# A two-layer graph attention kernel: sines in pairs later, weight matrices earlier, and the normalised rows' stores on another queue

## The chip, the cores and the metric

The kernel runs on one core of a Trainium2 chip. The metric is the time on the device in microseconds, the median of several runs. A profile is one execution of its own, recorded instruction by instruction; its durations are used for the working, and its total is not the median of the timed runs.

## The reference, cut to what matters

There are N = 6250 nodes with 128 features, and E = 106250 edges sorted by their target node (`dst`). Two transformer convolutions follow each other, with a normalisation over all nodes between them and a layer norm over the sum with x at the end.

```python
def _transformer_conv(h, edge_attr, src, dst, Wq, bq, Wk, bk, Wv, bv, We, Ws, bs):
    q, k, v = ...                      # h @ W + b, two heads of 64
    e = (edge_attr @ We).reshape(-1, H, C)
    kj = k[src] + e
    alpha = einsum('ehc,ehc->eh', q[dst], kj) / sqrt(C)
    a = softmax of alpha over the edges of each dst
    out = segment_sum((v[src] + e) * a[:, :, None], dst, num_segments=n)
    return out.reshape(n, H * C) + h @ Ws + bs

rel_t = last_update[src] - t
rel_t_enc = cos(rel_t[:, None] * time_w[None, :] + time_b)      # 32 values an edge
edge_attr = concatenate([rel_t_enc, msg], axis=-1)              # 32 + 64
h = _transformer_conv(x, edge_attr, src, dst, ...layer 1...)
h = relu((h - mean over nodes) / sqrt(var over nodes + 1e-5) * bn_g + bn_b)
h = _transformer_conv(h, edge_attr, src, dst, ...layer 2...)
x = layernorm(x + h)
```

## The kernel before, in words

**Tiling.** The edges are cut into NC = 106 chunks of CE = 1024 edges, each with the edges of at most NN = 64 nodes. A chunk lies in SBUF as eight tiles of 128 edges (`ff`, 241 columns). Instead of q, k and v of each edge, the kernel makes for each node a column per head (the "table", `ftab`), against which the raw features of the source nodes and the edge attributes are multiplied. The tables are made in 13 blocks of 512 nodes (`tables`, lines 622 to 638) as products of small matrices with the node features; `matrices` (574 to 605) makes these matrices from the weights once for each layer: three transposes (L580), then four pairs of products (L595 a matrix, L599 a column), each emptied from PSUM by ACT (L597) and DVE (L601).

**A round.** `conv(c, extra, first_blocks)` runs over both layers (c = 0 and 1) with a loop over k from -4 to NC + 2. The order of instructions on each engine is the order in which the program issues them (`manual_schedule`). Round k holds, for different chunks: `fetch(k + 4)`, which has SP read the chunk's node and edge offsets (L722, L723) and issue its loads (edge attributes L725, table L736, in layer 2 also the encodings `fz` L739, the turned attributes `fxT` L741 and the residual rows `fr` L743); `gather(k + 4)`, eight indirect loads by POOL (L748); `score(k, 0)` and `score(k, 1)` on PE (L817, L818); `turn_weights(k - 1)`, transposes and ACT copies (L840, L841); `divide(k - 2)` on DVE (L852 to L855); `finish_turn(k - 2)` (L867, L868, L870); `lowest(k)` on DVE (L823, L825); `turn_in(k + 1)` (L797 to L807); `weigh(k)`, the exponential on ACT (L830); in layer 1 the encoding of times; a pull of the generator `extra`; `finish(k - 2)`; and `gather_sums(k - 1)` on PE (L847). PE's transposes in `turn_in`, `turn_weights` and in the extra work share four PSUM banks in rotation.

**Sines.** `encode` makes the arguments of the cosine of one chunk on DVE (L765 to L773), `sine` has ACT evaluate them (L779), `place` copies them into the chunk and has SP store them for layer 2 (L784, L785). Up to round SINGLE = 16 each round encodes chunk k + 2 and takes its sine at once. In round SINGLE it encodes both k + 2 and k + 3. From then on it encodes chunk k + 3 and takes one sine for two chunks. ACT loads another function table whenever it goes from exponentials to a sine and back; a load stands in the profile at the line of the function that needs it.

**Extra work of layer 1.** `rest()` is a generator from which each round pulls one step, two steps in rounds 0 to 3 and after round 80. It makes the table blocks 1 to 12 (five steps each, then two in which weights for layer 2 are loaded by `load_others`, while it has any), then layer 2's matrices (seven steps), then for each of 13 blocks of 512 rows `pass_rows`: turn the rows of the finished layer back (L1002, L1004), take their statistics (L992) and store them in `h_d` from SP's queue (L1012, L1014). A block of rows waits for the round in which its last node is finished.

**The seam between the layers.** After layer 1, scale and shift are worked out (L1035 to L1044), and block 0 of the table of layer 2 is made. Then `conv(1, ...)` begins. At k = -4 it fetches and gathers chunk 0, and calls `first_blocks`: ACT normalises the other 12 blocks of `fhT` in place (L1074), PE turns each block of 512 nodes into rows (L1002), DVE copies them out of PSUM into one of three buffers `fhr` (L1004), and they are stored in `hn_d` (L1012, the last 106 rows by L1014), in the kernel before from ACT's queue. Chunks 0 to 2 (k < RAW = 3) gather their rows from `h_d`, not normalised, and are normalised by ACT while they are turned (L799). Chunks from 3 on gather from `hn_d`, so POOL's gather of chunk 3 needs all its stores landed.

Of the kernel before, what the change touches and what calls it, by code (L numbers as in the profile page):

```python
# [13 lines left out]
P = 128  # L14
# [646 lines left out]
def ordered(ctx: ExitStack, tc: tile.TileContext, pl, x, dst, edge_attr_64, conv2, bn_g, bn_b, out):  # L661


    nc = tc.nc
    N = x.shape[0]
# [26 lines left out]

    AHEAD = 4

    SINGLE = 16

    RAW = 3

    def conv(c, extra, first_blocks=None):
# [221 lines left out]
        def pull(gen, n):  # L921
            for _ in range(n):
                next(gen, None)

        with cs, tc.manual_schedule():
            for k in range(-AHEAD, NC + 3):
                def on(j):
                    return 0 <= j < NC

                if on(k + AHEAD):  # L930
                    fetch(k + AHEAD)
                    gather(k + AHEAD)
                if k == -AHEAD and c:
                    first_blocks()
                if on(k):
                    score(k, 0)
                if on(k - 1):
                    turn_weights(k - 1)
                place()
                if on(k - 2):  # L940
                    divide(k - 2)
                if on(k):
                    score(k, 1)
                if on(k - 2):
                    finish_turn(k - 2)
                if on(k):
                    lowest(k)
                if on(k + 1):
                    turn_in(k + 1, 0)
                if on(k):  # L950
                    weigh(k)
                if on(k + 1):
                    turn_in(k + 1, 1)
                for j in (k + 2,) if k < SINGLE else (k + 2, k + 3) if k == SINGLE else (k + 3,):
                    if c == 0 and on(j):
                        encode(j)
                        if j < SINGLE + 3:
                            sine()
                if k >= 0:
                    at_round[0] = k  # L960
                    pull(extra, 2 if k < 4 or k > 80 else 1)
                if len(args) == 3 or args and k == NC - 4:
                    sine()
                if on(k - 2):
                    finish(k - 2)
                if c and on(k):
                    if k < RAW:
                        normalise(k)
                    nc.vector.tensor_copy(ch[k].f[:, :, 1 + D:1 + D + TD], ch[k].z)
                for _ in range(min(len(done), 2 if k > NC - 12 else 1)):  # L970
                    store(*done.pop(0))
                if on(k - 1):
                    gather_sums(k - 1)
            at_round[0] = 2 * NC
            for _ in extra:
                pass
            for rows in done:
                store(*rows)
# [4 lines left out]
    with tc.tile_pool(name="fpw", bufs=2) as pw:  # L983
        with tc.tile_pool(name="ftp", bufs=3, space=bass.MemoryType.PSUM) as mp, tc.manual_schedule():
            turn_features(nc, pl, mp, N)

        def pass_rows(b0):

            r0 = b0 * GE
            n = min(GE, N - r0)  # L990
            rows = turned_rows(b0)
            nc.vector.bn_stats(stats[:, b0], hT[:, r0:r0 + n])  # L992
            yield
            put_rows(nc.sync, h_d, b0, rows)
            yield

        def turned_rows(b0):
            r0 = b0 * GE
            n = -(-min(GE, N - r0) // P)
            pt = pl.bank().rearrange("p (b d) -> p b d", d=P)  # L1000
            for i in range(n):
                nc.tensor.transpose(pt[:, i], hT[:, r0 + i * P:r0 + (i + 1) * P], ident)  # L1002
            rows = pw.tile([P, GE // P, P], F32, name="fhr", bufs=3)
            nc.vector.tensor_copy(rows[:, :n], pt[:, :n])  # L1004
            return rows

        def put_rows(eng, to, b0, rows):
            r0 = b0 * GE
            n = min(GE, N - r0)
            full = n // P  # L1010
            if full:
                eng.dma_start(to[r0:r0 + full * P, :].rearrange("(b p) d -> p b d", p=P), rows[:, :full])  # L1012
            if n > full * P:
                eng.dma_start(to[r0 + full * P:N, :], rows[:n - full * P, full])  # L1014

        def rest():
            others = load_others(nc, pl, const, conv2, bn_g, bn_b)
            for b0 in range(1, NT):
                yield from tables(nc, pl, 0, xT[:, b0 * GE:(b0 + 1) * GE], b0, pw, lambda: pl.bank())

                for _ in range(2):
                    next(others, None)
                    yield
            yield from matrices(nc, pl, 1, const, lambda: pl.bank()[:, :P])
            for b0 in range(-(-N // GE)):

                while at_round[0] < 3 + max(k for k in range(NC) if first(k)[0] < (b0 + 1) * GE):
                    yield
                yield from pass_rows(b0)

        conv(0, rest())


        moments = const.tile([P, 2], F32, name="fmom")
        nc.vector.bn_aggr(moments, stats)  # L1035
        std = const.tile([P, 1], F32, name="fstd")
        nc.vector.tensor_scalar(std, moments[:, 1:], EPS, None, op0=OP.add)
        nc.scalar.activation(std, std, AF.Sqrt)
        scale = pl.scale = const.tile([P, 1], F32, name="fscale")
        nc.vector.reciprocal(scale, std)  # L1040
        nc.vector.tensor_mul(scale, scale, pl.bng)
        shift = pl.shift = const.tile([P, 1], F32, name="fshift")
        nc.vector.tensor_mul(shift, scale, moments[:, 0:1])
        nc.vector.tensor_sub(shift, pl.bnb, shift)  # L1044

        def residual(b0):

            r0 = b0 * GE
            xr = pw.tile([P, 4, D], F32, name="fxr")
            n = min(GE, N - r0)  # L1050
            full = n // P
            if full:
                nc.scalar.dma_start(xr[:, :full], x[r0:r0 + full * P, :].rearrange("(b p) d -> p b d", p=P))
            if full < 4:
                nc.vector.memset(xr[:, full:], 0.0)
                nc.scalar.dma_start(xr[:n - full * P, full], x[r0 + full * P:N, :])
            yield
            pg = pl.bank().rearrange("p (b d) -> p b d", d=D)
            for i in range(4):
                nc.tensor.matmul(pg[:, i], hT[:, r0 + i * P:r0 + (i + 1) * P], pl.ws[1], start=True, stop=True)  # L1060
            nc.vector.tensor_add(xr, xr, pg)
            nc.vector.tensor_add(xr, xr, pl.bs2[:, None, :].to_broadcast([P, 4, D]))
            nc.scalar.dma_start(res_d[r0:r0 + GE, :].rearrange("(b p) d -> p b d", p=P), xr)

        def block(b0):
            res = residual(b0)
            next(res)
            yield from tables(nc, pl, 1, hT[:, b0 * GE:(b0 + 1) * GE], b0, pw, lambda: pl.bank())
            next(res, None)
            yield  # L1070

        def relu(b0):
            r = slice(b0 * GE, (b0 + 1) * GE)
            nc.scalar.activation(hT[:, r], hT[:, r], AF.Relu, bias=shift, scale=scale)  # L1074

        def first_blocks():

            for b0 in range(1, NT):
                relu(b0)
            for b0 in range(-(-N // GE)):  # L1080
                put_rows(nc.scalar, hn_d, b0, turned_rows(b0))

        with tc.tile_pool(name="fpp2", bufs=3, space=bass.MemoryType.PSUM) as pp, tc.manual_schedule():
            pl.bank = lambda: pp.tile([P, GE], F32, name="fpg")
            relu(0)
            for _ in block(0):
                pass

            diag = const.tile([P, 2, P], F32, name="fdiag")
            spread = pl.spread = const.tile([P, 2, P], F32, name="fspread")  # L1090
            pb = pp.tile([P, 2, P], F32, name="fpb", bufs=1)
            for i, col in enumerate((scale, shift)):
                nc.vector.tensor_scalar(diag[:, i], ident, col, None, op0=OP.mult)
                nc.tensor.matmul(pb[:, i], pl.ones, diag[:, i], start=True, stop=True)
            nc.vector.tensor_copy(spread, pb)

        def rest():
            for b0 in range(1, NT):
                yield from block(b0)
                yield  # L1100
                yield

        conv(1, rest(), first_blocks)
# [214 lines left out]
```

## Time and profile before

| | us |
|---|---|
| median of 3 runs | 2816.28 (2807.70 to 2822.51) |
| the profiled execution, its own time | 2308.59 |
| its span, first to last instruction | 2306.8 |
| mean granted TensorE clock in it | 0.980 |
| layer 1, rounds 0 to 105 (exponentials) | 67.3 to 1178.3 |
| seam, from the last exponential of layer 1 to the first of layer 2 | 1178.3 to 1241.1 |
| layer 2, first exponential to the last | 1241.1 to 2283.9 |

How to read it: PE is TensorE's matmuls and PEld its weight loads, DVE is VectorE, ACT ScalarE, POOL GpSimd, SP SyncE. `L817` is line 817 of the kernel. A row such as `fps<-fft,ftab` names the tile written and those read. "Idle before" in brackets is the time that an engine stood still ahead of an instruction, with the work that ended it. The profiled execution is shorter than the timed runs by 18%; the working below says how the two are set against each other.

### The profile page before, as it was taken

Reading aid. Unit: us, or ns where it says so; the run is one execution under the profiler, and the core shown is the slowest. Engines: PE = TensorE matmul, PEld = TensorE weight load, DVE = VectorE, ACT = ScalarE, POOL = GpSimd, SP = SyncE. Lnnn points to the kernel's source line nnn. Section 1 sums busy time; section 2 is a strip of 40 time slices with the busy share of each in tenths; the row PEclk is TensorE's granted clock in tenths of the full one; section 3 lists DMA queues with packets and bytes.
Section 4 is the critical chain, followed back from the end, with each engine's and each line's share of the span. In section 5 each row is a group of like instructions: output and inputs, shape, how many; then the busy total and the mean of one; then the engine's idle time right before and its main releaser. Section 6 shows DMA issues by size and latency. Waiting matters only on the chain. (4 is left out here: it accounts for less than half of the span.)

```text
span 2306.8 us, 39033 instructions
## 1 busy us (share of the span) xinstructions
PE 2214.9 (96%) x11586; PEld 1711.8 (74%) x11586; DVE 1240.1 (54%) x3738; ACT 1195.2 (52%) x1919; POOL 1629.7 (71%) x1717
## 2 busy tenths in 40 slices
PE   5999999999999999999977999999999999999997
PEld 3688788888887888788854777777777777776775
DVE  5676676767676767687734343434343334433333
ACT  3677565656666665555642344444444444443444
POOL 3777777777777777677616777777777777777772
PEclk7999999999999999999997999999999999999999
DMA  7666566666666566566628766677666776666561
GB/s 233 170 179 177 155 180 187 174 160 179 189 174 183 156 191 178 134 184 177 161 87 233 188 179 174 180 185 189 183 179 173 185 189 178 177 161 163 156 156 39
DMA packets 431067, 396.58 MB, mean 172 GB/s; under 512 B 279649, under 2 KB 375134, under 8 KB 427518
## 3 DMA queue, kind: packets, MB, share of 16 engines
q1 hardware_dynamic: 351188, 236.53, 37.0%
q0 software_dynamic: 54656, 113.07, 20.4%
q10 hardware_dynamic: 25002, 44.40, 5.5%
q8 instruction: 95, 1.56, 0.3%
q14 instruction: 126, 1.03, 0.1%
HBM read 277.19 MB, written 113.17 MB: 169 GB/s over the span
## 5 line engine op out<-in xcount | busy, mean ns | idle before, releaser
L748 POOL DMA_INDIRECT ff<-xv_d,fsrcs x848 | 819.3, 966 | 313.5 <-issue 220.9
L748 POOL DMA_INDIRECT ff<-hn_d,fsrcs x824 | 782.6, 950 | 261.6 <-issue 216.4
L847 PE MATMUL fpa<-ff,fpt 128*128 128x225 f32 x3392 | 694.9, 357 | 0.0
L847 PEld LDWEIGHTS fpa<-ff,fpt 128*128 128x128 f32 x3392 | 628.9, 190 | 11.8 <-issue 1.0
L841 ACT COPY fpt<-fppt 128x512 f32<-128x512 f32 x424 | 227.7, 589 | 503.8 <-PE fppt L840 492.4
L817 PE MATMUL fps<-fft,ftab 128*128 128x512 f32 x848 | 443.5, 605 | 3.7 <-ACT fft L799 2.1
L801 ACT COPY fft<-fpx 128x512 f32<-128x512 f32 x418 | 243.3, 582 | 365.7 <-PE fpx L797 365.7
L870 DVE COPY fat<-fpo 128x256 f32<-128x256 f32 x212 | 90.1, 425 | 590.1 <-PE fpo L868 584.3
L830 ACT ACTIVATE fs<-fps,fm 128x1024 f32<-128x1024 f32 x212 | 236.3, 1115 | 84.3 <-DVE fm L825 81.8
L840 PEld LDWEIGHTS fppt<-fident,fs 128*128 128x128 f32 x1696 | 198.5, 140 | 104.8 <-issue 104.3
L797 PE MATMUL fpx<-fident,ff 128*128 128x128 f32 x1696 | 248.2, 276 | 20.1 <-DMA ff<-hn_d,fsrcs 11.2
L823 DVE TENSOR_REDUCE flow<-fps 128x1 f32<-128x1024 f32 x212 | 257.5, 1215 | 11.4 <-PE fps L818 11.4
L797 PEld LDWEIGHTS fpx<-fident,ff 128*128 128x128 f32 x1696 | 198.6, 142 | 31.8 <-DMA ff<-hn_d,fsrcs 19.1
L840 PE MATMUL fppt<-fident,fs 128*128 128x128 f32 x1696 | 220.1, 272 | 0.0
L818 PE MATMUL fps<-fxT,ftab 112*128 112x512 f32 x424 | 218.4, 596 | 0.0
L818 PE MATMUL fps<-fet,ftab 112*128 112x512 f32 x424 | 217.1, 593 | 0.0
L817 PEld LDWEIGHTS fps<-fft,ftab 128*128 128x128 f32 x848 | 166.6, 226 | 7.4 <-ACT fs L830 3.3
L818 PEld LDWEIGHTS fps<-fet,ftab 112*128 112x128 f32 x424 | 106.3, 251 | 75.8 <-issue 58.2
L818 PEld LDWEIGHTS fps<-fxT,ftab 112*128 112x128 f32 x424 | 84.1, 198 | 99.9 <-issue 99.2
L772 DVE SCALAR_TENSOR_TENSOR farg<-fturns,farg 128x256 f32<-128x256 f32 x318 | 135.4, 426 | 10.9
L852 DVE TENSOR_SCALAR finv<-fpa 128x1 f32<-128x1 f32 x212 | 32.5, 153 | 196.1 <-DMA ff<-hn_d,fsrcs 88.7
L806 PE MATMUL fpe<-fident,ff 128*112 128x128 f32 x848 | 130.1, 277 | 2.8 <-DVE ff L784 1.5
(202 smaller groups left out, 2309.0 us busy)
## 6 DMA issues: line engine op xcount, KB each, us to landing
ff<-in_edge_attr SPq DMA_DIRECT2D x212, 256.0 KB
et_d<-fet SPq DMA_DIRECT2D x106, 448.0 KB
fxT<-et_d SPq DMA_DIRECT2D x106, 448.0 KB
ftab<-tab_d SPq DMA_DIRECT2D x106, 192.0 KB
tab_d<-fo ACTq DMA_DIRECT2D x13, 1536.0 KB
ff<-xv_d,fsrcs POOLq DMA_INDIRECT x848
enc_d<-fzs SPq DMA_DIRECT2D x106, 128.0 KB
ftab<-tab_d SPq DMA_DIRECT2D x106, 128.0 KB
```

The lines of the kernel that those rows point to most:

```text
L748: nc.gpsimd.indirect_dma_start(out=f[:, t, (1 if c else 0):1 + D], out_offset=None, in_=(h_d if k < RAW else hn_d) if c else pl.xv_d, in_o ...
L772: nc.vector.scalar_tensor_tensor(arg, turn, -part, arg, op0=OP.mult, op1=OP.add)
L797: nc.tensor.transpose(px[:, t * P:(t + 1) * P], s.f[:, u * 4 + t, 1:1 + D], ident)
L801: nc.scalar.copy(s.ft[:, u * GE:(u + 1) * GE], px)
L806: nc.tensor.transpose(pe[:EC, t * P:(t + 1) * P], s.f[:, u * 4 + t, 1 + D:], ident)
L817: nc.tensor.matmul(s.ps[:, w], s.tab[:, :, 0], s.ft[:, w], start=True, stop=False)
L818: nc.tensor.matmul(s.ps[:, w], s.tab[:EC, :, 1], s.et[:, w], start=False, stop=True)
L823: nc.vector.tensor_reduce(low, s.ps, AX.X, OP.min)
L830: nc.scalar.activation(s.s, s.ps, AF.Exp, bias=s.bias, scale=-1.0)
L840: nc.tensor.transpose(pp[:, t * P:(t + 1) * P], s.s[:, at:at + P], ident)
L841: nc.scalar.copy(s.pt[:, u * GE:(u + 1) * GE], pp)
L847: nc.tensor.matmul(s.pa, s.pt[:, t * P:(t + 1) * P], s.f[:, t, 1:1 + D + EW], start=t == 0, stop=t == T - 1)
```

## The change

SINGLE goes from 16 to 40. The matrices of layer 2 are made in the steps that `load_others` leaves empty between the table blocks, not after them; and rounds pull two steps after round 96 only, not after round 80. `put_rows` issues all its stores from SP's queue, those of `hn_d` too, which come in the program after the loads of chunk 0 and ahead of those of chunk 1; and it cuts the last 106 rows into two stores of 96 and 10.

```diff
-    SINGLE = 16
+    SINGLE = 40
...
-                    pull(extra, 2 if k < 4 or k > 80 else 1)
+                    pull(extra, 2 if k < 4 or k > 96 else 1)
...
-            put_rows(nc.sync, h_d, b0, rows)
+            put_rows(h_d, b0, rows)
...
-        def put_rows(eng, to, b0, rows):
+        def put_rows(to, b0, rows):
             r0 = b0 * GE
             n = min(GE, N - r0)
             full = n // P
             if full:
-                eng.dma_start(to[r0:r0 + full * P, :].rearrange("(b p) d -> p b d", p=P), rows[:, :full])
-            if n > full * P:
-                eng.dma_start(to[r0 + full * P:N, :], rows[:n - full * P, full])
+                nc.sync.dma_start(to[r0:r0 + full * P, :].rearrange("(b p) d -> p b d", p=P), rows[:, :full])
+
+            left = n - full * P
+            for a, b in ((0, left // 16 * 16), (left // 16 * 16, left)):
+                if a < b:
+                    nc.sync.dma_start(to[r0 + full * P + a:r0 + full * P + b, :], rows[a:b, full])
 
         def rest():
-            others = load_others(nc, pl, const, conv2, bn_g, bn_b)
+            def second():
+                yield from load_others(nc, pl, const, conv2, bn_g, bn_b)
+                yield from matrices(nc, pl, 1, const, lambda: pl.bank()[:, :P])
+
+            others = second()
             for b0 in range(1, NT):
                 yield from tables(nc, pl, 0, xT[:, b0 * GE:(b0 + 1) * GE], b0, pw, lambda: pl.bank())
 
                 for _ in range(2):
                     next(others, None)
                     yield
-            yield from matrices(nc, pl, 1, const, lambda: pl.bank()[:, :P])
+            yield from others
...
             for b0 in range(-(-N // GE)):
-                put_rows(nc.scalar, hn_d, b0, turned_rows(b0))
+                put_rows(hn_d, b0, turned_rows(b0))
```

## The prediction

> **What bounds the kernel now.** I read the page first, for who is busy, then the time of each stage, then the timeline where a stage is slow. On the page PE stands at 9 tenths or more in all slices but the first, two in the middle and the last, and PEclk below 9 only in the first and once at the middle.
>
> ```profile
> PE 2214.9 (96%) x11586; PEld 1711.8 (74%) x11586; DVE 1240.1 (54%) x3738; ACT 1195.2 (52%) x1919; POOL 1629.7 (71%) x1717
> PE   5999999999999999999977999999999999999997
> PEclk7999999999999999999997999999999999999999
> ```
>
> Stages, cut where a round's exponential (L830) starts; columns are length, busy us of each engine (with counts), granted clock, DMA share, GB/s:
>
> ```profile
> 92.88:239.94 147.06, 147.06 (x783) 118.90 (x782) 101.99 (x299) 110.97 (x147) 111.85 (x116) 1.00 0.67 189
> 239.94:290.27 50.33, 45.18 (x222) 35.50 (x221) 32.61 (x96) 28.69 (x40) 37.37 (x39) 0.93 0.54 143
> 290.27:436.54 146.27, 146.27 (x779) 118.12 (x778) 102.64 (x299) 89.70 (x126) 108.47 (x112) 1.00 0.63 177
> 916.40:976.63 60.23, 56.54 (x288) 46.51 (x287) 35.96 (x111) 28.96 (x47) 38.19 (x40) 0.91 0.51 130
> 1207.00:1232.00 25.00, 9.79 (x49) 6.91 (x47) 7.84 (x17) 1.70 (x3) 14.69 (x16) 0.64 1.10 311
> ```
>
> The first is rounds 2 to 16 with one sine a round, the third is rounds 20 to 34 with one for two: 10.50 and 10.45 us a round, PE never idle. The three others lose time: the switch to pairs, layer 2's matrices, the seam between the layers. The timeline names what PE, ACT or POOL waited for there (in brackets, us and releaser):
>
> ```profile
> 255.41 0.17 DVE L765 TENSOR_TENSOR frel<-ff,few 128x8 f32<-128x8 f32 x1 [4.42 <-DMA ff<-xv_d,fsrcs]
> 262.73 0.45 PE L867 MATMUL fpo<-fident,fa 128*128 128x128 f32 x1 [3.05 <-DVE fa L855]
> 938.28 0.79 PE L595 MATMUL fpg<-ftr,ftr 64*128 64x128 f32 x2 [2.50 <-ACT fft L801]
> 953.73 0.48 PE L595 MATMUL fpg<-ftr,ftr 64*128 64x128 f32 x2 [1.18 <-ACT fft L801]
> 1230.92 1.45 ACT L799 ACTIVATE fft<-fpx,fshift,fscale 128x512 f32<-128x512 f32 x2 [23.30 <-DMA hn_d<-fhr]
> 1236.96 0.94 POOL L748 DMA_INDIRECT ff<-hn_d,fsrcs  x1 [10.71 <-DMA fr<-res_d]
> ```
>
> **Which time is compared.** The profiled execution took 2308.6 us (span 2306.8), the runs shown 2816.28 in the median, 22% more. [...] So I cost each part twice, at the profile's clock[...].
>
> [...] PE's clock falls to half[...]: gaps of 3.05 and 2.50 us were enough (L867 takes 0.45 instead of 0.27; after 938.28 the L847 group's weights take 4.73 us instead of 2.96), 2.10 us at 248.8 was not. [...] The trace has the 1283[...] (load 265.78, exponential 267.08). [...]
>
> **Part a, SINGLE 40.** Rounds 17 to 40 make 24 sines of 0.507 instead of 12 of 0.722 (+3.5), with 12 more sine and 12 more exponential loads: 24 x 1.283 = 30.8. That is 34.3 us on ACT, 1.43 a round. The cover is PE's round: ACT goes from 89.70/14 = 6.4 to 7.8 us of 10.45, and the first stage ran so (110.97/14 = 7.9) with PE full. Cost 0; bounds 0 and 34.3. What moves is the switch. Rounds 17 to 20 took 50.33 where 4 x 10.45 = 41.8 were due: 8.5 lost. Two encodings in one round (3.3 us each on DVE) hold back L855, for which PE waits 2.10; next round L765 waits 4.42 for gathers one chunk earlier than before, and L867 3.05, then the half clock. At round 40 POOL, with 8 x 1.25 = 10.0 us a chunk against 10.45, has gained 24 x 0.45 = 10.8 more, over 4.42: that wait and the slow clock go, the first gap stays (1.5, as round 17 took 12.18 where 10.69 is usual for such a round). Gain 7.0. [...]
>
> **Part b, the matrices.** From 916.40 five rounds took 60.23; three short and two long ones are 3 x 8.8 + 2 x 10.9 = 48.2 (rounds 95 to 98 alternate so). PE's own work added is 3.8 (three transposes at 0.11, four L595 pairs at 0.49, four L599 pairs at 0.28, one turned block at 0.43). So 8.2 lost: 3.7 of waits, 4.5 of slow clock. The waits come with the second product of a round, which needs a PSUM bank that ACT empties only after the exponential; the first one of a round (935.18) waits for nothing. The change puts one product at most in each of rounds that had an empty pull, and a gap of a few tenths costs no clock. Gain 8.2. [...] The load of the matrices is long landed. Blocks of rows now go one pull a round from round 80: the same PE and DVE work, the last four still bound to rounds 91, 99, 107 and 108, SP's stores one round apart. Cost 0.
>
> **Part c, the seam.** Moved: 12 stores of 256 KB and the 106 rows, now two stores, from ACT's queue to SP's behind chunk 0's five loads. ACT no longer waits 23.3; its L799 waits only for PE. SP reaches the first store at 1209.2 (chunk 0's last load, 1208.66 + 0.54), 2.0 later than ACT's 1207.18. Before, 13 stores took until 1230.9, three in flight (three buffers) and 5.5 us each, beside loads in 16 full DMA engines: 25 us x 311 GB/s = 7.8 MB, of which 3 x 0.99 = 3.0 MB are loads of chunks 1 to 3. These now queue behind the stores; 4.8 MB take 15.4 us. I estimate 3.4 us a cycle of three stores once chunk 0's loads are out of the way: last issue 1224.5, landed 1227. PE's first transposes of layer 2 need the banks of the tenth and eleventh copy, so scoring starts at 1222.5 instead of 1231.75, and POOL's gather of chunk 3 at 1227.5 instead of 1236.96. Late next: chunk 1's loads. SP needs 3.2 for the two values ahead of a chunk, 2 more to its fxT, and 0.99 MB take 3.2: landed at 1233, when PE is at 1222.5 + 10.5 = 1233. No margin there; at chunk 2 there are 2 us. I take 9.0 in the profile, where POOL paces the end (rounds of 10.0, PE's 9.28), so POOL's gain is the one that counts[...] (bounds: gain 11, loss 6). The extra store costs SP 0.3 to 0.5, and the split can take up to 2 off the tail of the 106 rows (issue 1192.65, first gather 1196.46). PE waits for neither: 0.
>
> **Sum.** Profile: 7.0 + 8.2 + 9.0 = 24.2, so 2308.6 becomes 2284. Median: 0 + 6.2 + 8.8 = 15.0, so 2816.28 becomes 2801.3.
>
> **Rivals.**
> 1. *The profile's gains whole in the timed runs*, because they are slow for another reason than PE's clock: 24.2 to 28 us, 2788 to 2792. For it: no view here shows the timed runs' clock. [...]
> 2. *The seam gives nothing back*: SP is late for chunk 1 by what ACT gains, because the 16 engines stay full whatever the order. Only part b is left: 2810. For it: share 1.10 and no margin at chunk 1.
> 3. *Slower: ACT's table loads reach PE* in rounds 17 to 40. The place is the copy L841 behind the sine: PE's banks come free late. Price up to 34.3, less 15.0: 2835. It decides from 15.0, that is, once 44% of the 34.3 lands on PE. Against: the first stage, 10.50 a round with the same loads. For: there the matrices' copies were not on ACT too.
> That the stores do not move is excluded: in the built program SP has all 14 between chunk 0's and chunk 1's loads.
>
> **How the numbers follow.** My case has 0.55, rival 1 0.2, rival 2 0.15, rival 3 0.1. About what a measurement tells from no change is 0.5%, 14.1 us. My case spreads from 2794 to 2809 over its bounds, so 0.33 of its 0.55 lie beyond 14.1, with rival 1 0.53 faster; the rest of it and rival 2 give 0.36 the same; rival 3, and a seam at its worse bound with the spread of a median (7 us), 0.11 slower. The range 2782 to 2819 holds my case, rival 1 with 6 of spread and rival 2 with 9, and leaves out rival 3.
>
> **What would show it.** Right: about 2284 in the profile; 12 more L779 and 12 more L830 loads, rounds 17 to 40 at 10.45; rounds near 82 without waits on L595 and at full clock; L799's wait of 23.3 gone, first L817 of layer 2 some 9 us earlier after layer 1's end, the gather of chunk 3 too. Wrong: PE idle behind ACT in rounds 17 to 40, L818 waiting for fxT at chunk 1, or a stall as large at round 41 as at 17.

## The result, and the profile after

The kernel after takes 2779.84 us in the median of 6 runs (2759.72 to 2826.6), the kernel before 2815.71 (2807.7 to 2825.36): ratio 0.988, 95% interval 0.984 to 0.993. It is faster, by 36 us in the medians (19 to 46 by the interval). The ratio leaves out one of the six runs after, 2826.6, which was a slow one. The forecast was 2801.3. The median lies 2 us below the lower end of its range, 2782; the ratio, applied to 2816.28, gives 2784, just inside.

The page of the kernel after (2784.45 us, span 2782.7, granted clock 0.948): engines, then PE's busy share and granted clock by slice, then PE's costliest group (busy us, mean ns of one).

```profile
PE 2353.5 (85%) x11586; PEld 1744.2 (63%) x11586; DVE 1258.1 (45%) x3738; ACT 1241.9 (45%) x1955; POOL 1618.6 (58%) x1717
...
PE   4598898989998898888866988888888988888887
...
PEclk7699999999999999999987999999999999999999
...
L847 PE MATMUL fpa<-ff,fpt 128*128 128x225 f32 x3392 | 704.0, 361 | 1.8 <-issue 1.8
```

Set beside the profile before, PE's share falls from 96% to 85%, yet one L847 takes 361 ns against 357 there. The clock that this trace records is full or half: half for 290 us, against 95 in the profile before. So this execution is not longer because PE's clock is lower throughout, as the prediction assumed for the timed runs. Of the 476 us between the two spans, 337 are PE standing still (15% of the span instead of 4%), and 139 are PE busy for longer, in part at half clock. The timeline shows one such halt (start, length, engine; in brackets the idle time before and what ended it):

```profile
917.78 0.14 PEld L840 LDWEIGHTS fppt<-fident,fs 128*128 128x128 f32 x1 [0.52 <-issue]
919.15 0.01 SPq L725 DMA_DIRECT2D ff<-in_edge_attr  x1
919.18 0.49 PE L840 MATMUL fppt<-fident,fs 128*128 128x128 f32 x3 [1.67 <-issue]
...
919.25 0.58 ACT L807 COPY fet<-fpe 112x512 f32<-112x512 f32 x1 [4.43 <-remote]
919.33 0.54 DVE L883 TENSOR_TENSOR fres<-fpo,ftab 64x64 f32<-64x64 f32 x2 [3.65 <-remote]
...
919.80 0.94 POOL L748 DMA_INDIRECT ff<-xv_d,fsrcs  x1 [2.38 <-PE fppt L840]
```

PE, ACT, DVE and POOL start again within 0.7 us of each other, just as SP issues the edge load of a new chunk (L725), and the releasers shown for PE, ACT and DVE ("issue", "remote") are none of the kernel's tiles: "issue" stands for a wait that the profile does not explain, "remote" for a release that it cannot place.

Not every halt looks like this one. I call it a halt here when ACT, DVE and POOL stand still together for 1 us or more. The trace has 183 of them over its 212 rounds, 308 us in all; a trace of the same kernel without this trouble, shown below, has 14. PE stands still with them for as long in only 27 (39 us). PE's own gaps of 1 us or more are 149 (306 us), and in many of them the other engines work. Only 49 of the 183 end within 0.7 us of an L725. So the profile before and the profile after were not taken under the same condition, and can't be laid side by side. The experiments below supply the missing pairs.

### The profile page after: what moved, and what is told of

It is laid out like the page before. It is cut to its first block, busy times and chain, and to the rows that moved or that the text cites. A ratio compares the mean times of both kernels' runs of the same rounds, so it can differ in the third digit from the quotient of the medians.

```text
span 2782.7 us, 39082 instructions
## 1 busy us (share of the span) xinstructions
PE 2353.5 (85%) x11586; PEld 1744.2 (63%) x11586; DVE 1258.1 (45%) x3738; ACT 1241.9 (45%) x1955; POOL 1618.6 (58%) x1717
## 3 DMA queue, kind: packets, MB, share of 16 engines
q0 software_dynamic: 54656, 113.07, 15.3%
## 5 line engine op out<-in xcount | busy, mean ns | idle before, releaser
L847 PE MATMUL fpa<-ff,fpt 128*128 128x225 f32 x3392 | 704.0, 361 | 1.8 <-issue 1.8
L847 PEld LDWEIGHTS fpa<-ff,fpt 128*128 128x128 f32 x3392 | 636.3, 193 | 15.4 <-issue 2.7
L817 PE MATMUL fps<-fft,ftab 128*128 128x512 f32 x848 | 461.6, 623 | 62.5 <-ACT fs L830 30.5
L840 PE MATMUL fppt<-fident,fs 128*128 128x128 f32 x1696 | 252.5, 279 | 87.8 <-issue 75.2
L901 DVE SCALAR_TENSOR_TENSOR fres<-fpo,fr 64x128 f32<-64x128 f32 x106 | 29.9, 282 | 537.9 <-PE fppt L840 287.4
L905 ACT ACTIVATE fsq<-fy 64x128 f32<-64x128 f32 x106 | 32.8, 310 | 514.7 <-DVE fy L903 292.8
L830 ACT ACTIVATE fs<-fps,fm 128x1024 f32<-128x1024 f32 x212 | 236.3, 1115 | 58.2 <-issue 28.6
L818 PE MATMUL fps<-fxT,ftab 112*128 112x512 f32 x424 | 228.5, 619 | 8.9 <-issue 6.3
L797 PEld LDWEIGHTS fpx<-fident,ff 128*128 128x128 f32 x1696 | 206.6, 147 | 21.4 <-issue 19.1
L867 PEld LDWEIGHTS fpo<-fident,fa 128*128 128x128 f32 x212 | 30.2, 142 | 281.8 <-issue 209.5
L807 ACT COPY fet<-fpe 112x512 f32<-112x512 f32 x212 | 125.1, 590 | 152.9 <-remote 49.4
L867 PE MATMUL fpo<-fident,fa 128*128 128x128 f32 x212 | 63.0, 297 | 150.9 <-DVE fa L855 59.5
```

Of the source, the lines that this page charges most:

```text
L797: nc.tensor.transpose(px[:, t * P:(t + 1) * P], s.f[:, u * 4 + t, 1:1 + D], ident)
L807: nc.scalar.copy(s.et[:, u * GE:(u + 1) * GE], pe[:EC])
L817: nc.tensor.matmul(s.ps[:, w], s.tab[:, :, 0], s.ft[:, w], start=True, stop=False)
L818: nc.tensor.matmul(s.ps[:, w], s.tab[:EC, :, 1], s.et[:, w], start=False, stop=True)
L830: nc.scalar.activation(s.s, s.ps, AF.Exp, bias=s.bias, scale=-1.0)
L840: nc.tensor.transpose(pp[:, t * P:(t + 1) * P], s.s[:, at:at + P], ident)
```

## The experiments

They fell on three chips. On two, the kernel before ran in 2303.93 (a first group of four runs) and 2307.49 (a second group), near the 2308.6 of its profile. On a third it ran in 2747.67, with the halts. I call the first two quiet. Each group ran on one chip at one time, so chip and time are not told apart, and on which chip the runs of the result fell is not on record.

### Each part alone, and single sines throughout

The first quiet chip. Part a alone, on the kernel before:

```diff
-    SINGLE = 16
+    SINGLE = 40
```

> Part a alone: the kernel before with SINGLE 40 in place of 16; matrices and stores as before. The prediction's theory (rounds are paced by a slow PE clock in the timed runs, ACT's extra loads are covered, the switch swallows its own gap): 0, so 2816 and a ratio of 1.000. Theory of the trace after (the rounds are stretched by stalls of all engines together and not by the clock; there rounds 5 to 40 with one sine each took 12.10 us, rounds 40 to 100 with one for two took 12.87): 24 x 0.77 = 18 us less, 2798, ratio 0.993. Rival 3 of the prediction (ACT's 34.3 us reach PE): up to 34 us more, ratio 1.012.

Measured: 2303.91 against 2303.93, ratio 1.000 (0.999 to 1.001). No difference.

Part b alone:

```diff
-                    pull(extra, 2 if k < 4 or k > 80 else 1)
+                    pull(extra, 2 if k < 4 or k > 96 else 1)
...
-            others = load_others(nc, pl, const, conv2, bn_g, bn_b)
+            others = second()
...
-            yield from matrices(nc, pl, 1, const, lambda: pl.bank()[:, :P])
+            yield from others
```

> Part b alone: the kernel before with layer 2's matrices beside layer 1's table blocks and the second pull from round 97; SINGLE 16 and the stores on ACT as before. The prediction: 6.2 us less (bounds 3 and 9), ratio 0.998. Rival: in rounds of 12 us or more the waits of rounds 81 to 84 lie inside stalls that come anyway, and the part gives 0, ratio 1.000. Slower, by up to 5 us, if the products that now stand beside the table blocks meet the second product of a round elsewhere.

Measured: 2297.61, ratio 0.997 (0.996 to 0.998): 6.3 us less.

Part c alone (the new `put_rows`, and):

```diff
-                put_rows(nc.scalar, hn_d, b0, turned_rows(b0))
+                put_rows(hn_d, b0, turned_rows(b0))
```

> Part c alone: the kernel before with the normalised rows' stores (and the cut of the last rows' store) issued by SP ahead of the loads of chunks 1 to 3; SINGLE 16 and the matrices as before. The prediction: 8.8 us less (bounds: 11 less, 6 more), ratio 0.997. Rival 2 (SP is late for chunk 1 by what ACT gains): 0, ratio 1.000. From the trace after, where from the last exponential of layer 1 to the first of layer 2 it took 66.15 us against 62.80 in the profile before, and the next two rounds 19.7 and 20.6 against 7.3 and 10.5: up to 20 us more, ratio 1.007, if that is due to the stores and not to the stalls.

Measured: 2296.28, ratio 0.997 (0.995 to 0.998): 7.65 us less. In its trace the seam took 54.14 us against 62.8 in the profile before, not longer as the third guess had it; that guess had read the halts.

Single sines in all of layer 1, on the kernel after:

```diff
-    SINGLE = 40
+    SINGLE = 1000
```

> The changed kernel with SINGLE over the number of chunks: one sine a round throughout layer 1, the switch to pairs is gone. Theory of the trace after: the rounds from 40 to 103 lose 0.77 us each and the switch at 41 its 5 us: 50 less than the kernel after, about 2730, ratio to before 0.970. The prediction's theory: ACT's loads are covered, so only the switch counts: 0 to 8 less than the kernel after, ratio 0.985 to 0.988. Rival 3: from round 40 ACT's 1.43 us a round reach PE: up to 90 us more than the kernel after, ratio 1.02.

Measured: 2284.16, ratio 0.991 (0.990 to 0.993). ACT's busy time grows from 1194.6 (part c alone) to 1314.3, and the kernel is no slower than the kernel after with its ratio of 0.993 (next section): rival 3 falls for all of layer 1, not only for rounds 17 to 40. The 0.77 us a round did not show on the quiet chip.

### The two kernels again, on one quiet chip

> The changed kernel itself, once more, beside the parts' condition (before 2304 here, not 2816). Theory: the parts add up (a 0.0, b 6.3, c 7.65 as measured alone): 14.0 less, ratio 0.994; the 1.2% of the result (0.988) then belongs to the stretched condition, where a round with pairs cost 0.77 us more than one with single sines. Rival: the parts are worth more together (the stall of one had hidden the gain of another): 0.988 here too, that is 27 us less.

> The kernel before itself, for its profile beside those of the parts. Theory: the switch at rounds 17 to 20 takes 46.5 us as in the two parts that keep SINGLE at 16, not the 50.33 of the profile that the prediction read, so the profile's 8.5 lost was not the usual toll. Rival: 50.3 again, and the parts changed the switch. Whole: 2304, or 2816 if the stretched condition comes back.

The second quiet chip. The kernel after: 2290.3 against 2307.49, ratio 0.993 (0.991 to 0.994), 17.2 us less. The parts alone sum to 14.0; their intervals and this one overlap, so they add up as far as these runs tell. The kernel before, run once for its profile: 2303.36. That is less than each of its nine timed runs there (2305.03 to 2308.55), so the two profiles below differ by 13.1 us where the medians differ by 17.2.

Now the stages can be compared. Rounds 16 to 20, 40 to 44, 80 to 86, 98 to 100, the seam (105 to 106) and 106 to 108, cut at the exponentials; columns as in the prediction. Before:

```profile
240.05:288.79 48.74, 43.69 (x222) 34.57 (x221) 32.66 (x96) 28.71 (x39) 37.18 (x38) 0.96 0.54 145
497.50:539.36 41.86, 41.86 (x227) 34.21 (x226) 29.48 (x86) 25.04 (x35) 30.42 (x32) 1.00 0.66 192
...
914.93:984.00 69.07, 65.07 (x354) 53.86 (x353) 45.33 (x138) 36.38 (x57) 46.75 (x49) 0.98 0.53 146
1105.50:1125.67 20.17, 20.17 (x114) 16.74 (x113) 15.45 (x45) 11.74 (x17) 15.24 (x17) 1.00 0.57 162
1173.80:1235.26 61.46, 37.19 (x151) 24.59 (x149) 22.20 (x52) 18.52 (x25) 25.79 (x28) 0.75 0.63 185
1235.26:1253.01 17.75, 16.61 (x81) 11.54 (x80) 11.57 (x21) 8.95 (x12) 13.79 (x14) 1.00 0.73 219
```

After:

```profile
240.32:282.29 41.97, 41.97 (x222) 33.38 (x221) 29.03 (x86) 31.05 (x43) 32.00 (x33) 1.00 0.60 159
493.50:538.20 44.70, 42.79 (x231) 34.69 (x230) 33.46 (x98) 28.30 (x40) 30.75 (x33) 1.00 0.61 181
...
913.76:974.07 60.31, 60.31 (x338) 50.29 (x337) 45.36 (x133) 35.22 (x51) 45.90 (x48) 1.00 0.63 172
1095.14:1117.48 22.34, 20.32 (x114) 16.74 (x113) 15.02 (x45) 11.73 (x17) 17.05 (x18) 1.00 0.67 187
1165.62:1219.54 53.92, 35.17 (x151) 23.55 (x149) 21.84 (x52) 18.63 (x24) 24.88 (x27) 0.78 0.54 156
1219.54:1241.18 21.64, 17.36 (x81) 11.39 (x80) 11.67 (x21) 8.81 (x12) 16.76 (x17) 1.00 1.13 255
```

Read in pairs, these rows hold most of the change: with rounds 20 to 40 they make 11.7 of the 13.1 us between the two spans (2301.6 and 2288.5 us). The old switch gives 6.8 us and the new one takes 2.8 (0.7 of that is matrix work that now falls here, as in part b alone; between 20 and 40 another 2.5 us of it: 208.71 became 211.21). The matrices give 8.8. At rounds 98 to 100, 2.2 are lost with the same work on PE. The seam gives 7.5, and rounds 106 to 108, at a DMA share of 1.13, take 3.9 back. Rounds 44 to 80 take 375.57 and 375.56.

Where the 2.2 go is one line of PE's timeline of the kernel after:

```profile
1106.15 0.33 PE L1002 MATMUL fpg<-fident,fhT 128*128 128x128 f32 x1 [2.02 <-DMA fhT<-fres]
```

The eleventh block of rows is turned there; its last columns come back from a 32 KB store that SP issued at 1100.72. In the kernel before the same transposes pass without a wait: the store that they need was issued at 1110.69.

```profile
1114.00 0.67 PE L1002 MATMUL fpg<-fident,fhT 128*128 128x128 f32 x4
```

### What the seam is worth, and to whom

Same chip, on the kernel after. The stores moved behind chunk 1's loads, and a fourth buffer of rows:

```diff
-                if k == -AHEAD and c:
+                if k == 1 - AHEAD and c:
```

> The changed kernel with the normalised rows' stores issued by SP behind chunk 1's loads too (ahead of chunks 2 and 3's alone). Theory of the prediction's last step (chunk 1's loads have no margin behind the stores, and POOL's gather of chunk 3 sets what the seam is worth): PE's wait for chunk 1's fxT (1.55 us in part c alone, in a round of 11.6 instead of 7.25) goes, but the stores and the gather of chunk 3 come 4 to 5 later: 0 to 5 us slower than the kernel after, ratio to before 0.994 to 0.996. Rival: PE's lateness at chunk 1 is what costs, and POOL has slack: 2 to 4 faster than the kernel after, ratio 0.992.

```diff
-        def turned_rows(b0):
+        def turned_rows(b0, fourth=False):
...
-            rows = pw.tile([P, GE // P, P], F32, name="fhr", bufs=3)
+            if fourth:
+                rows = pl.xT[:, 6 * CE:6 * CE + GE].rearrange("p (b d) -> p b d", d=P)
+            else:
+                rows = pw.tile([P, GE // P, P], F32, name="fhr", bufs=3)
...
-                put_rows(hn_d, b0, turned_rows(b0))
+                put_rows(hn_d, b0, turned_rows(b0, b0 % 4 == 3))
```

> The changed kernel with a fourth buffer of normalised rows (in a part of the encodings' memory that is free by then), so that four stores can be in flight. Theory: the stores go at the pace of their flight, three at a time (12 took 15.7 us from first to last issue in part c alone): with four 11.8, all of the seam some 3 to 4 us earlier, ratio to before 0.992. Rival: the 16 DMA engines are full (share over 1 at the seam), and a fourth store waits in them: 0 against the kernel after, ratio 0.994.

Measured: chunk 1 first 2295.72, ratio 0.995 (0.993 to 0.996), 5.4 slower than the kernel after; four buffers 2287.95, ratio 0.992 (0.990 to 0.993), 2.4 faster, at the edge of what these runs tell. A few lines of each timeline say why: SP's twelve stores, POOL's first gather of `hn_d`, PE's scores of chunk 1. The kernel after:

```profile
1197.36 15.72 SPq L1012 DMA_DIRECT2D hn_d<-fhr  x12
...
1216.75 0.95 POOL L748 DMA_INDIRECT ff<-hn_d,fsrcs  x1 [4.18 <-DMA hn_d<-fhr]
...
1223.57 1.13 PE L818 MATMUL fps<-fxT,ftab 112*128 112x512 f32 x2 [1.73 <-DMA fxT<-et_d]
```

Chunk 1's loads first:

```profile
1206.70 15.81 SPq L1012 DMA_DIRECT2D hn_d<-fhr  x12
...
1225.81 0.94 POOL L748 DMA_INDIRECT ff<-hn_d,fsrcs  x1 [8.66 <-DMA hn_d<-fhr]
...
1232.17 1.02 PE L818 MATMUL fps<-fxT,ftab 112*128 112x512 f32 x2
```

Four buffers (the timeline splits its stores into several rows; the text below has their times):

```profile
1214.68 0.95 POOL L748 DMA_INDIRECT ff<-hn_d,fsrcs  x1 [2.40 <-DMA hn_d<-fhr]
...
1220.71 1.14 PE L818 MATMUL fps<-fxT,ftab 112*128 112x512 f32 x2 [1.62 <-DMA fxT<-et_d]
```

With chunk 1 first PE's wait of 1.73 is gone, as foretold, but POOL waits 4.48 more for `hn_d`, and the kernel loses. Only part of the 5.4 us can be seen at the seam: from layer 1's last exponential to layer 2's last, this profile takes 1.5 more than that of the kernel after, and 3.3 lie in layer 1, which the edit does not touch. The nine quiet traces together say it better. Where the stores went from ACT (four traces), POOL's gather of chunk 3 came 57.2 to 59.7 us after layer 1's last exponential, and layer 2's last exponential 1105.2 to 1106.9 after it. Where they went from SP ahead of chunk 1 (four), it was 49.3 to 51.1 and 1097.8 to 1100.1. Chunk 1 first lies between, 55.4 and 1101.6, though its PE does not wait. So the worth of the seam goes with POOL's gather and not with chunk 1.

With a fourth buffer the stores are issued from 1196.64 to 1210.3 (13.7 instead of 15.7, where 11.8 was expected), and from the last exponential of layer 1 to that of round 108 it takes 72.40 instead of 75.56. So the buffers paced part of the stores. That the transfers pace the rest is not shown.

### The halves of part b, and two versions meant to be faster

These four fell on the chip with the halts. Part b's two edits apart, on the kernel before: only the matrices moved, and only the pull's bound.

> Half of part b: the kernel before with layer 2's matrices beside layer 1's table blocks, but the second pull still from round 81. Theory: part b's gain at rounds 81 to 85 was partly given back at the end of round 98, where PE waited 2 to 3 us for a store of sums that SP had queued behind 256 KB of rows; with two pulls the rows are out by round 93, and that wait goes: 8.5 to 9 us less than before, ratio 0.996 (part b whole: 0.997, rounds 98 to 100 in 23.39 us; here 20.2). Rival: the pace of the rows has nothing to do with that wait: ratio 0.997 and rounds 98 to 100 in 22 to 23 us.

> The other half of part b: the kernel before with the second pull from round 97 only; the matrices stay behind the table blocks, from round 81. Theory of the prediction (PE waits there only with the second product of a round): no waits of 2.50 and 1.18 on L595, rounds 80 to 86 in about 64 us instead of 69.1, but the matrices now take eight rounds and the rows start later, so that six or more blocks of rows are left for the rounds from 97: 0 to 4 us less than before, ratio 0.998 to 1.000. Rival: the products wait wherever they stand so late, one a round too: rounds 80 to 86 as before, ratio 1.000 to 1.002.

Measured: matrices alone 2740.06 against 2747.67, ratio 0.998 (0.996 to 1.001); bound alone 2732.3, ratio 0.994 (0.991 to 0.996). In the profile of the matrices alone the rows are out early, and still PE waits 2.76 us at rounds 98 to 100 for the store of sums, against my theory of the loss there. But this profile has the halts, and so does not decide it. The nine quiet traces all fit the theory: in the five whose second pull starts at round 97, a 256 KB store of rows was issued 0.6 to 0.7 us ahead of that store of sums and PE waits 0.7 to 3.1 us; in the four where it starts at round 81, no store of rows is ahead and PE does not wait. It stays open whether the rows ahead are the whole cause, since the halves of part b were not run apart on a quiet chip.

For the matrices, the kernel before on the quiet chip has these lines in PE's timeline, the first and the second product of a round:

```profile
933.71 0.48 PE L595 MATMUL fpg<-ftr,ftr 64*128 64x128 f32 x2
...
936.80 0.48 PE L595 MATMUL fpg<-ftr,ftr 64*128 64x128 f32 x2 [2.50 <-ACT fft L801]
```

and of the kernel with the bound alone the trace answers for L595 (all that PE and its weight loads waited there, us and times):

```profile
L595 PE MATMUL fpg<-ftr,ftr x8: 272/322/373, 1130.2 to 1167.8; 64*128 64x128 f32 x8
its engine sat idle before it (us, times) until:
  issue: 0.7, 4
```

The first product of that round, at 933.71, waits for nothing, and so it is in the other round with two (none, then 1.18). With the bound alone there is one product a round, and it waits for nothing on ACT, though it stands where it stood. The halts lengthen the rounds there; but in the kernel after on the quiet chip, with one product a round beside the table blocks, the four wait for ACT 0.7 us together. So it was the second product of the round that waited. Why this half gained 15 us in the medians here, which no theory had, is not shown; the two profiled executions differ by 0.8 us in span.

Single sines throughout with four buffers of rows, and the same with the second pull from round 81 again:

> The changed kernel with one sine a round throughout layer 1 and a fourth buffer of normalised rows, the two edits that each ran faster than it. Theory: they touch different stretches and add up: 0.9911 x 0.9917 / 0.9929 = 0.990, 23 us less than before. Rival: POOL's pace in layer 2 takes back what the seam gains, and only the singles are left: 0.991.

> As the one before, with the second pull from round 81 again in place of 97. Theory (a store of sums behind 256 KB of rows at round 98): rounds 98 to 100 shorter by 1 to 2 us (21.0 with single sines throughout; 19.7 is what two rounds take there without a wait), ratio 0.989. Rival: no difference from the one before, 0.990.

Measured: 2698.51, ratio 0.984 (0.981 to 0.987), and 2697.2, ratio 0.982 (0.979 to 0.985). Between them nothing can be told, and rounds 98 to 100 were not shorter with the earlier pull (25.2 against 23.9). Both gain twice the 23 us that were expected. The stretch from round 44 to 80, without any switch in it, shows where. The kernel with the matrices moved (pairs from 16):

```profile
646.76:1095.88 449.12, 397.17 (x1998) 312.27 (x1997) 267.89 (x767) 232.54 (x321) 275.26 (x289) 0.97 0.54 148
```

Single sines, four buffers:

```profile
631.23:1060.95 429.72, 385.02 (x1998) 300.45 (x1997) 275.31 (x767) 282.58 (x375) 276.73 (x289) 1.00 0.56 154
```

The same 1998 matmuls take 12.2 us less of PE, at a clock of 1.00 instead of 0.97, and PE idles 7.3 less; on a quiet chip this stretch is 375.6 either way. In rounds 20 to 40 it is 239.51 at 1.00 against 254.71 at 0.95 (247.66 at 0.96 with the bound alone), and the kernel after itself, with its single sines there, has 242.83 at 1.00. In these stretches with halts, pairs lose clock and single sines do not. PE's longest gaps in them are 3.6 to 4.0 us with pairs and at most 1.75 with single sines. Pairs alone are not enough for it: in rounds 86 to 98 they keep 0.99 to 1.00.

## Why the prediction was right or wrong

**Which time is compared: wrong.** The second prices, 0, 6.2 and 8.8, rest on an assumption of mine that no trace shows: that in the timed runs PE's clock is lower throughout by a fixed share, and the other engines keep their pace. The trace after has the clock at full or half, 0.948 in the mean, and most of its extra time is PE standing still. The condition came and went with the group of runs, under the same program. So they priced rounds that do not exist. Rival 1 named the right doubt ("slow for another reason than PE's clock").

**Part a.** Cover: right. 12 more loads each on L779 and L830 (62 to 74, 75 to 87), ACT 31.05 us in rounds 17 to 20 and PE full at 41.97. The switch: the mechanism was right, since at round 41 the second gap is gone and the first stays (1.91 us in the kernel after, 2.27 in part a alone, 1.5 predicted). The size of 7.0 was not: the 8.5 came from one execution. In four profiles without halts the switch at 16 cost 8.4 (the profile read), 6.8, 4.6 and 4.5 over the 41.97 that rounds 16 to 20 take without one. In four others it cost 4.1, 2.1, 3.8 and 2.1 at 40, over the 41.86 that rounds 40 to 44 take without one (42.59 with matrix work in them). Alone the part measured 0.0, within 2.3 us. So "0" was the figure in the sum for the wrong reason. With halts the part also has a gain that I had not seen, the clock of rounds 20 to 40 (1.00 against 0.95 and 0.96), some 5 to 12 us in those traces; against it the kernel after took 55.95 for rounds 40 to 44, where the two kernels with pairs took 47. These traces come from two groups of runs, so the balance is not shown.

**Part b.** 8.2 and 6.2 predicted, 6.3 measured. That the 6.2 came so near is no merit of its working, which rests on the lower clock. The loss at rounds 81 to 84 varies from one execution to the next: rounds 80 to 85 took 60.23, 57.70, 57.66 and 60.76 in the four quiet profiles that have the matrices there, so by the prediction's own sum 8.2, 5.7, 5.7 and 8.8 were lost. That only the second product waits was right. That a gap of a few tenths costs no clock holds in the profile that the prediction read: from 2050 to 2260 PE's gaps of 0.2 to 0.7 us left it at 1.00. The step that failed is "SP's stores one round apart. Cost 0": rounds 98 to 100 became 2.2 longer (3.2 in part b alone). I had priced the stores and not the eleventh block's wait for its sums.

**Part c.** 9.0 predicted, 7.65 measured. From layer 1's last exponential (part c alone, 1174.25) the first store went 31.2 later (30.9 predicted), 12 stores took 15.7 (15.3), the gather of chunk 3 came 50.66 later where 49.24 was due: before it was 58.70, so POOL gained 8.0 of the 9.5 reckoned. "Chunk 1's loads, no margin": PE waited 1.55 there. That POOL's gain is what counts held when chunk 1's loads went first. With halts less of the gain is seen: from round 105 to 108, 106.44 in the kernel after (another group of runs) and 103.9 in the two kernels with four buffers, against 107.24 and 107.84 with the stores on ACT.

**The sum.** For the profile's condition 24.2 was predicted; on a quiet chip 17.2 came (13 to 20 by the interval), and from the parts alone 0, 6.3 and 7.65. What was missing is mostly the switch, then 1 to 2 each of b and c. In the runs recorded, 15.0 was predicted and 36 came. I can't divide the 36: of the parts, only the halves of b were run with halts, and in another group of runs; and the quiet chip's 0.993 lies at the edge of the interval. That 15.0 came nearer to the 17.2 of the quiet chip than 24.2 did is luck: its 0 for part a and its 6.2 for part b rest on a clock lower throughout that no trace has. The direction was right; that it was larger where the halts are fits the clock of single rounds, which is not enough to call it shown.

## What to carry to other kernels

A loss read from one execution (a stall with its slow clock after it, here 8.4 us at the switch against 4.5 to 6.8 in three others) can be twice the usual one: look at the same stretch in a second profile before counting on getting it back. When timed runs are far longer than the profile, the profile can't tell why; price only what it shows, and ask for a trace of the slower condition. A store moved earlier is worth what the last waiter gets: here POOL's gather, while the loads displaced behind it took half of the gain back in the next two rounds.

## What the runs showed that I had not expected

The kernel before took 2304 and 2307 us on two chips and 2748 on a third, with the same program. With the halts, ACT, DVE and POOL stand still together 143 to 183 times in the five traces, for 1.6 to 1.7 us in the median, and SP's own instructions around L725 look different. Its rows for L725's load (ns: least, median, most), in the kernel after on a quiet chip:

```profile
L725 SPq DMA_DIRECT2D ff<-in_edge_attr x212: 384/407/431, 36.1 to 2226.5; - x106
```

and in the recorded execution of the kernel after:

```profile
L725 SPq DMA_DIRECT2D ff<-in_edge_attr x212: 2/18/1398, 37.1 to 2726.7; - x106
```

The issue that always took 0.4 us takes anything from 2 ns to 1.4 us. What stops the engines is not shown; no experiment reached it. In the five traces with halts PE's clock in the rounds from 20 to 40 and from 44 to 80 is 0.95 to 0.97 with pairs and 1.00 with single sines; why is not shown.

When the clock falls, the length of a gap alone does not tell. In the profile before, the 2.50 us ahead of 938.28 were followed by half clock (0.50 from 938.2 to 944), and so were the 1.18 ahead of 953.73 (0.50 from 956 to 958); the 2.10 ahead of 248.80 were not (1.00 from 244 to 259.6). In the recorded execution of the kernel after PE stood still for 2.70 us ahead of 1065.36, and the clock stayed at 1.00 (1058 to 1072). So a gap of 2 us can cost the clock or not; what decides it is not shown.
